# The scan pass of a vision state-space block: softplus in pairs, u*D as a matmul, a new order of work, and a part of x_proj moved into the pass

## The chip, the cores and the metric

The kernel runs on one core of one Trainium2 chip. The time is that of one execution on the device, in microseconds (us). The kernel before takes 10042.06 us, the median of three runs (10038.65 to 10054.98). A core has five engines that work side by side, each through its own queue of instructions in order: TensorE (PE in the profile; PEld is its weight load), VectorE (DVE), ScalarE (ACT), GpSimd (POOL), and SyncE (SP), which here only issues DMAs.

## What is computed

The reference is a selective state-space block with four scan directions on a batch of 8 images of 64 x 64 pixels, followed by a small attention and a feed-forward layer. Only the scan and what feeds it matter here. `B` is 8, `L` is 4096 pixels, `D_INNER` is 192 channels, `D_STATE` (n) is 16, `DT_RANK` is 6, `K` is 4 directions:

```python
x_dbl = jnp.einsum('bkdl,kcd->bkcl', xs, x_proj_weight)         # "x_proj": 6 + 16 + 16 rows
dts, Bs, Cs = x_dbl[:, :, :6], x_dbl[:, :, 6:22], x_dbl[:, :, 22:]
delta = jax.nn.softplus(dt_projs_weight @ dts + bias)            # [b, k, d, l]
h = h * jnp.exp(d_t[..., None] * A) + (d_t * u_t)[..., None] * b_t[:, :, None, :]
y = jnp.einsum('bkdn,bkn->bkd', h, c_t)                          # at each step of l
y = y + D[None, :, :, None] * u
```

The first three lines are abridged; the last three are the recurrence for one step, its output, and the term u*D, which is added once per direction.

## The kernel before

`vss_attn_ffn_kernel` calls three passes. `pass1` (line 266) norms the input, projects it, convolves it on VectorE and stores the result `u` to HBM (`u_d`); then `x_projection` (line 490) computes x_proj with TensorE, copies it out of PSUM and stores it to `xd_d`, and `split` (line 236) splits B and dt into three bf16 parts (`b_d`, `dt_d`). `pass3` does the norm, gate, output projection, attention and feed-forward.

`pass2` (line 542) is the scan. It works through 192 **pieces**: 4 pairs of images, in each pair 3 channel groups `c` (c = 0 and 1 are 128 channels of one image; c = 2 holds the last 64 channels of both), 4 directions `k`, and 4 chunks of T = 1024 pixels. A piece has 16 states n. For each n:

- `decay` (line 655): ACT makes `da` = exp(delta * A_n), 128x1024;
- `products` (line 694): the term delta*u*B_n is made in a PSUM tile `wide` in one of three ways, set by `WAYS` (line 55). Either PE spreads B_n over the partitions and DVE multiplies by `du`; or ACT (`scaled`, line 665) or POOL (`scaled_by_pool`) multiplies the transposed `duT` by B_n, which gives `x` or `xg`, and PE transposes that into `wide`;
- `scan` (line 718): one DVE instruction runs the recurrence along the 1024 pixels and writes `h`;
- for every two n: `times_c` (line 757), where POOL multiplies `h` by a loaded, broadcast tile `c`, and `sum_over_n` (line 771), where PE adds the result into the PSUM tile `acc`.

`prepare` (line 573) readies a piece: loads of `xdt`, `xb` and `u`, the B transposes, `delta` by a softplus on ACT, `du` on POOL, `duT`. Softplus and the exponential lie in different activation tables, so ACT loads a table before a softplus and another after it. For direction 0, `sum_over_n` starts `acc` with u*D: ACT multiplies (`ud`), PE transposes.

The order on each engine is fixed when the kernel is built. `weave` (line 142) takes generators that yield (engine, cost, delay, slots), keeps a clock per engine, and always emits the step that can begin first by those written costs; ties go to the lower rank (`lead` in the list of units). `room` (line 550) is the number of buffers of each kind: 3 `da`, 3 `h`, 3 `x`, 3 `wide`, 6 `c`.

The batches from `LATE` = 5 on are split during pass 2, in between (`late_split`). All of x_proj lies in pass 1; its last batch has half of its PSUM copies on DVE.

Of the kernel before, what the change touches and what calls it, by code (L numbers as in the profile page):

```python
# [33 lines left out]
F32 = mybir.dt.float32  # L34
# [20 lines left out]
WAYS = [([2, 5, 6, 8, 11, 12, 14, 15], [3, 7]), ([2, 3, 7, 9, 14], [0, 5, 12])]  # L55
NS = 3

LATE = 5
GRP = 512
# [40 lines left out]
@with_exitstack  # L100
def vss_attn_ffn_kernel(ctx: ExitStack, tc: tile.TileContext, g: dict, out: bass.AP):
    nc = tc.nc
    consts = ctx.enter_context(tc.tile_pool(name="consts", bufs=1))
    dram = ctx.enter_context(tc.tile_pool(name="scratch", bufs=1, space=DRAM))

    ident = consts.tile([P, P], F32, name="ident")
    make_identity(nc, ident)
    mhalf = consts.tile([P, NBLK], F32, name="mhalf")
    nc.vector.memset(mhalf, -0.5)


    u_d = [[dram.tile([DI, L], F32, name=f"u_d{b}_{o}") for o in range(2)] for b in range(NB)]

    y_d = [[dram.tile([L, DI], F32, name=f"y_d{b}_{o}") for o in range(2)] for b in range(NB)]
    z_d = [dram.tile([DI, L], F32, name=f"z_d{b}") for b in range(NB)]
    xd_d = [[dram.tile([2 * NXD, L], F32, name=f"xd_d{b}_{o}") for o in range(2)] for b in range(NB)]

    b_d = [[dram.tile([2, NS, N, L], BF16, name=f"b_d{b}_{o}") for o in range(2)] for b in range(NB)]
    dt_d = [[dram.tile([2, NS, R, L], BF16, name=f"dt_d{b}_{o}") for o in range(2)] for b in range(NB)]

    engines = [InOrder(tc, e) for e in (nc.tensor, nc.vector, nc.scalar, nc.gpsimd)]
    fixed, load_dt_w = scan_constants(tc, g, consts, dram, ident)
    pass1(tc, g, load_dt_w, ident, mhalf, engines, u_d, z_d, xd_d, b_d, dt_d)
    pass2(tc, g, ident, engines, fixed, u_d, xd_d, b_d, dt_d, y_d)
    pass3(tc, g, ident, mhalf, engines, y_d, z_d, out)


class Slots:


    def __init__(self, count):
        self.count, self.taken, self.ends = count, 0, {}

    def when(self):

        return 0.0 if self.taken < self.count else self.ends.get(self.taken + 1 - self.count)
# [99 lines left out]
def split(engines, pool_of, cost, src, row, rows, pieces, at, dst):  # L236

    act, pool, sp = engines
    wide, used = GRP, rows * pieces
    yield "sp", 0.7, 4.0  # L240
    bq = pool_of.tile([P, wide], F32, name="bq")
    src = src[row : row + rows].rearrange("r (s t) -> (r s) t", s=pieces)
    sp.dma_start(bq[0:used], src[:, at : at + wide])
    yield "act", 0.6
    bs = pool_of.tile([P, NS, wide], BF16, name="bs")
    act.copy(bs[0:used, 0, :], bq[0:used])
    yield "pool", cost
    pool.tensor_sub(bq[0:used], bq[0:used], bs[0:used, 0, :])
    yield "act", 0.6
    act.copy(bs[0:used, 1, :], bq[0:used])  # L250
    yield "pool", cost
    pool.tensor_sub(bs[0:used, 2, :], bq[0:used], bs[0:used, 1, :])
    yield "sp", 0.9
    half = used // 2
    for k2 in range(2):
        to = dst[k2].rearrange("e n (s t) -> (n s) e t", s=pieces)[:, :, at : at + wide]
        sp.dma_start(to, bs[half * k2 : half * (k2 + 1)])
# [8 lines left out]
def pass1(ctx, tc, g, load_dt_w, ident, mhalf, engines, u_d, z_d, xd_d, b_d, dt_d):  # L266
# [28 lines left out]
    w_xp = wp.tile([P, 3, 2, P], F32, name="w_xp")  # L295
# [194 lines left out]
    def x_projection(b, o, q):  # L490
# [15 lines left out]
        by_dve = b == NB - 1 and q % 2 == 1  # L506
        end = yield ("dve" if by_dve else "act"), 0.6 if o == 0 else 0.8
# [4 lines left out]
        (dve.tensor_copy if by_dve else act.copy)(dst, src)  # L512
# [10 lines left out]
    for pair in range(NB // 2):  # L523
        batches = (2 * pair, 2 * pair + 1)
        for b in batches:
            units += [("stats", statistics(b, q)) for q in range(NG)]
            units.append(("norm", group_norm(b)))
            units += [("proj", projection(b, q)) for q in range(NG)]
        for c in ORDER:
            units.append(("conv", convolution(pair, c)))  # L530
        for b in batches:
            for o in range(2):
                units += [("xproj", x_projection(b, o, q)) for q in range(NG)]
                if b < LATE:
                    units += [("split", after(("xd", b, o), split((act, pool, sp), two, 4.4, xd_d[b][o], *w))) for w in splits(b, o, b_d, dt_d)]
# [6 lines left out]
def pass2(ctx, tc, g, ident, engines, fixed, u_d, xd_d, b_d, dt_d, y_d):  # L542
# [5 lines left out]
    one = ctx.enter_context(tc.tile_pool(name="p2one", bufs=1))  # L548
    two = ctx.enter_context(tc.tile_pool(name="p2two", bufs=2))
    room = {"c": 6, "da": 3, "h": 3, "x": 3, "wide": 3, "xg": 1, "ud": 1, "acc": 1}  # L550
# [8 lines left out]
    done, counts, made, ys, carry = {}, {}, {}, {}, {}  # L559
# [13 lines left out]
    def prepare(at):  # L573
# [10 lines left out]
        yield "sp", 2.5, 3.0  # L584
        xdt = one.tile([2 * NS * NS * R, T], BF16, name="xdt")
        queue = sp if at else pool
        for j in range(2):
            for m in range(NS):
                row = (j * NS + m) * NS * R
                queue.dma_start(xdt[row : row + NS * R, :], dt_d[2 * pair + j][o][k2].rearrange("s r t -> (s r) t")[:, cols])  # L590
        if at > 0:
            yield "sp", 1.5, 3.0
# [18 lines left out]
        yield "pe", 0.9, 0.2, slots["wide"]  # L611
        pd, slot = take("wide", [P, T])
        for q in range(0, T, GRP):
            pe.matmul(pd[:, q : q + GRP], dt_w[:, c, k, :], xdt[:, q : q + GRP], start=True, stop=True)

        end = yield "act", 3.6, 0.2
        delta = two.tile([P, T], F32, name="delta")
        act.activation(delta, pd, AF.Softplus, bias=dt_b[:, c // 2, k : k + 1])
        slots["wide"].release(slot, end)
        made[at] = [xb, u, delta, None, None, bT]  # L620
        done["delta", at] = end
        end = yield "pool", 2.37, 0.2
        du = two.tile([P, T], F32, name="du")
        pool.tensor_mul(du, delta, u)
        made[at][3] = du
# [6 lines left out]
        made[at][4] = two.tile([P, NT, P], F32, name="duT")  # L632
        act.copy(made[at][4], pt)
        slots["wide"].release(slot, end)
        done["duT", at] = end

    def late_split(b, o, which):

        yield "scans", 0
        yield from split((act, pool, sp), one, 1.25, xd_d[b][o], *which)  # L640
        one_more(("split", b), 6, 0.0)

    def load_c(at, m):
        pair, c, k, pc = pieces[at]
        parts = chunk_rows(pair, c)
        end = yield "sp", 0.5 * len(parts), 6.0, slots["c"]
# [8 lines left out]
    def decay(at, n):  # L655
# [3 lines left out]
        end = yield "act", 1.06, 0.2, slots["da"]  # L659
        da, slot = take("da", [P, T])  # L660
        act.activation(da, made[at][2], AF.Exp, scale=a_neg[:, c // 2, k, n : n + 1])
# [3 lines left out]
    def scaled(at, n):  # L665
# [3 lines left out]
        x, (_, _, _, _, duT, bT) = None, made[at]  # L669
        for i in range(0, NT, 2):  # L670
            cost = 0.6 if c < 2 else 1.0
# [9 lines left out]
    def scaled_by_pool(at, n):  # L681
        pair, c, _, _ = pieces[at]
        yield "duT", at
        end = yield "pool", 2.0 if c < 2 else 2.2, 0.2, slots["xg"]
        x, slot = take("xg", [P, NT, P])
        _, _, _, _, duT, bT = made[at]
# [7 lines left out]
    def products(at, n):  # L694
# [3 lines left out]
        if n in by_act or n in by_pool:  # L698
            yield "x", at, n
            end = yield "pe", 1.3, 0.2, slots["wide"]  # L700
# [5 lines left out]
        else:  # L706
            yield "du", at
            end = yield "pe", 0.7, 0.2, slots["wide"]
# [4 lines left out]
            end = yield "dve", 1.22, 0.0  # L713
            dve.tensor_mul(dbu, made[at][3], dbu)
# [3 lines left out]
    def scan(at, n):  # L718
# [6 lines left out]
        if n % 2 == 0:  # L725
            end = yield "dve", 2.26, 0.2, slots["h"]
            made["h", at, n // 2] = take("h", [P, 2, T])
            done["begun", at, n // 2] = 0.0
        else:
            yield "begun", at, n // 2  # L730
            end = yield "dve", 2.26, 0.2
# [39 lines left out]
    def sum_over_n(at, m):  # L771
# [10 lines left out]
        if m == 0 and k == 0:  # L782
            yield "delta", at
            yield "act", 1.05, 0.2, slots["ud"]
            ud, slot = take("ud", [P, T])
            act.mul(ud, made[at][1], dsum[:, c // 2 : c // 2 + 1])
            end = yield "pe", 1.2, 0.0, slots["acc"]
            made["acc"] = take("acc", [P, NT, P])
            add(ud, True, False)
            slots["ud"].release(slot, end)  # L790
# [10 lines left out]
        for i in range(2):  # L801
# [3 lines left out]
            else:  # L805
                end = yield "pe", 1.2, 0.0
# [5 lines left out]
    def take_acc(at):  # L812
# [11 lines left out]
        if k >= 2 and at % NPC == NPC - 1:  # L824
            yield "sp", 2.0, 6.0
# [13 lines left out]
    for at, (pair, c, k, pc) in enumerate(pieces):  # L839
# [5 lines left out]
        add("prep", 8, prepare(at))  # L845
        for n in range(N):
            if n % 2 == 0:
                add("c", 12, load_c(at, n // 2), n)
            add("da", 2, decay(at, n), n)
            if n in by_act:  # L850
                add("x", 5, scaled(at, n), n)
            elif n in by_pool:
                add("xg", 4, scaled_by_pool(at, n), n)
            add("dbu", 1, products(at, n), n)
            add("scan", 0, scan(at, n), n)
            if n % 2 == 1:
                if at % NPC < NPC - 1:
                    add("carry", -2, carries(at, n // 2), n)
                add("term", 0, times_c(at, n // 2), n)
                add("sum", -4, sum_over_n(at, n // 2), n)  # L860
        add("acc", 0, take_acc(at), N)
    last = [(b, o, w) for b in range(LATE, NB) for o in range(2) for w in splits(b, o, b_d, dt_d)]
    units += [("split", 5 * N * (i + 1), late_split(*which)) for i, which in enumerate(last)]
    weave(units, {"prep": 1, "c": 1, "da": 2, "x": 1, "xg": 1, "dbu": 2, "scan": 2, "carry": 1, "term": 1, "sum": 1, "acc": 1, "split": 1}, done)
# [301 lines left out]
```

## Time and profile before

| what | value |
|---|---|
| median of three runs | 10042.06 us |
| the profiled execution | 10032.78 us, span 10031.0 us |
| first scan starts (pass 1 until here) | 713.87 us |
| the last scan ends, pass 3 follows | 9313.4 us |
| DVE / ACT / POOL / PE busy, whole span | 95 / 92 / 90 / 74% |
| one piece, c = 0 or 1 (pair 1, c = 1: 703.4 us for 16) | 43.96 us |
| one piece, c = 2 (pair 1: 741.6 us for 16) | 46.35 us |

A stage of 16 pieces (one pair and one c) is cut at the end of the 16th scan of its last piece. In the page's list of groups, "busy" is the time in which at least one instruction of the group runs, and "mean" the time of one from start to end; where an engine starts an instruction before the last one has quite ended, the first is less than count times mean. "Idle" is the time just before the group's instructions in which the engine did nothing, with what ended it.

### The profile page before, as it was taken

To read this page: it belongs to the slowest core of one execution; us is meant where nothing else is said; L and a number is where in the kernel's file an instruction comes from. 1 tells how busy PE (TensorE), PEld (TensorE's weight loads), DVE (VectorE), ACT (ScalarE), POOL (GpSimd) and SP (SyncE) were. 2 spreads that over 40 slices of the span, in tenths; PEclk is the share of its full clock that TensorE was granted. 3 is DMA by queue.
4 is the path that set the end of the run, shared out by engine and by line. 5 is a ranking of instruction groups with operands and counts; after the bars stand their busy time and mean duration, and the time that the engine had idled before them with its cause. 6 is when DMAs were issued, how large, how long until landed. Compare 5 with 4: busy or idle time off the path is not lost.

```text
span 10031.0 us, 152994 instructions
## 1 busy us (share of the span) xinstructions
PE 7446.5 (74%) x52384; PEld 6168.3 (61%) x52384; DVE 9534.5 (95%) x7601; ACT 9182.1 (92%) x20692; POOL 9000.1 (90%) x2911
## 2 busy tenths in 40 slices
PE   7767777777777777777777777777777777777677
PEld 3336666666656666666666666666666666665566
DVE  7879999999999999999999999999999999999798
ACT  5669999999999999999999999999999999999687
POOL 1539999999999999999999999999999999999676
PEclk8889999998998999989999989999989999989898
DMA  5766676689986666799966766899866666999653
GB/s 166 234 212 216 223 237 222 227 212 205 209 223 213 224 221 213 223 209 204 212 215 216 232 209 221 220 203 204 223 209 226 216 215 223 211 204 209 186 171 104
DMA packets 932233, 2111.70 MB, mean 211 GB/s; under 512 B 274603, under 2 KB 422860, under 8 KB 929922
## 3 DMA queue, kind: packets, MB, share of 16 engines
q1 hardware_dynamic: 928650, 2100.57, 74.0%
q8 instruction: 419, 6.86, 0.3%
q14 instruction: 356, 2.92, 0.1%
q0 software_dynamic: 432, 0.94, 0.0%
q10 hardware_dynamic: 2376, 0.40, 0.0%
HBM read 1925.98 MB, written 175.66 MB: 210 GB/s over the span
## 4 chain that ended last, share of the span: by engine, by line
DVE 31%; ACT 29%; issue 15%; PE 13%; POOL 8%; DMA 3%; SPq 1%; DVEq 0%; ACTq 0%; POOLq 0%
DVE h L91 21%; ACT x L91 11%; ACT da L91 11%; POOL c L91 6%; PE acc L91 6%; DVE wide L91 5%; PE wide L91 3%; ACT L91 2%; ACT y L91 1%; DVE u L91 1%; PE pa L91 1%; ACT delta L91 1%; PE px L91 1%; DMA xd_d<-xd 1%; POOL xg L91 1%
## 5 line engine op out<-in xcount | busy, mean ns | idle before, releaser
L91 POOL TENSOR_TENSOR c<-c,h 128x2048 f32<-128x2048 f32 x1536 | 6960.6, 4558 | 293.2 <-issue 134.2
L91 DVE TENSOR_TENSOR_SCAN h<-da,carry,wide 128x1024 f32<-128x1024 f32 x2304 | 5267.9, 2332 | 135.1 <-PE wide L91 35.7
L91 ACT ACTIVATE x<-duT,bT 128x128 f32<-128x128 f32 (+1 forms) x13312 | 3969.8, 368 | 2.0
L91 PE MATMUL acc<-ident,c 128*128 128x128 f32 x24576 | 3419.1, 297 | 594.4 <-POOL c L91 587.9
L91 ACT ACTIVATE da<-delta,a_neg 128x1024 f32<-128x1024 f32 x3072 | 3512.7, 1144 | 318.0 <-DVE h L91 305.8
L91 PEld LDWEIGHTS acc<-ident,c 128*128 128x128 f32 x24576 | 3102.5, 154 | 1031.9 <-POOL c L91 921.7
L91 PE MATMUL wide<-ident,x 128*128 128x128 f32 x10752 | 1553.0, 290 | 650.4 <-DVE h L91 604.8
L91 PEld LDWEIGHTS wide<-ident,x 128*128 128x128 f32 x10752 | 1301.4, 149 | 845.0 <-ACT x L91 393.0
L91 DVE TENSOR_TENSOR_SCAN h<-da,wide 128x1024 f32<-128x1024 f32 x768 | 1713.1, 2271 | 41.5 <-PE wide L91 9.8
L91 DVE TENSOR_TENSOR wide<-du,wide 128x1024 f32<-128x1024 f32 x1280 | 1543.9, 1207 | 39.7 <-PE wide L91 39.2
L91 PE MATMUL wide<-xb,sel 96*128 96x512 bf16 x2560 | 820.2, 404 | 685.6 <-DVE h L91 671.0
L91 POOL TENSOR_TENSOR xg<-duT,bT 128x512 f32<-128x512 f32 (+1 forms) x640 | 895.2, 1414 | 26.5 <-PE wide L91 13.3
L91 PEld LDWEIGHTS <-sel 96*128 96x128 bf16 x2560 | 232.2, 102 | 867.0 <-DVE h L91 614.8
L91 PE MATMUL wide<-ident,xg 128*128 128x128 f32 x3584 | 482.3, 279 | 118.5 <-DVE h L91 116.7
L91 ACT ACT_TABLE_LOAD x386 | 495.2, 1283 | 25.9 <-DMA w_kv<-in_bqkv 19.2
L91 PEld LDWEIGHTS wide<-ident,xg 128*128 128x128 f32 x3584 | 411.4, 144 | 148.4 <-issue 108.4
L91 POOL TENSOR_TENSOR du<-delta,u 128x1024 f32<-128x1024 f32 x192 | 457.8, 2384 | 7.7 <-DMA u<-u_d 7.7
L91 DVE SCALAR_TENSOR_TENSOR u<-xpad,conv_w,u 128x4096 f32<-128x4096 f32 x96 | 454.5, 4734 | 1.9
L91 PE MATMUL px<-u,w_xp 128*128 128x512 f32 x512 | 253.4, 635 | 57.5 <-ACT u L91 42.2
L91 POOL TENSOR_TENSOR bq<-bq,bs 128x512 f32<-128x512 f32 (+1 forms) x48 | 125.7, 2623 | 162.7 <-ACT bs L91 123.7
L91 ACT COPY y<-acc 128x1024 f32<-128x1024 f32 x192 | 192.4, 1002 | 77.8 <-PE acc L91 77.6
L91 PE MATMUL wide<-ident,du 128*128 128x128 f32 x1536 | 206.5, 278 | 69.3 <-DVE h L91 34.9
(142 smaller groups left out, 5835.6 us busy)
## 6 DMA issues: line engine op xcount, KB each, us to landing
c<-xd_d SPq DMA_DIRECT2D x1024, 1024.0 KB
c<-xd_d SPq DMA_DIRECT2D x1024, 512.0 KB
u<-u_d SPq DMA_DIRECT2D x127, 512.0 KB
xdt<-dt_d SPq DMA_DIRECT2D x1146, 36.0 KB
xb<-b_d SPq DMA_DIRECT2D x382, 96.0 KB
u<-u_d SPq DMA_DIRECT2D x128, 256.0 KB
zs<-z_d SPq DMA_DIRECT2D x128, 256.0 KB
y_d<-y SPq DMA_DIRECT2D x24, 1024.0 KB
```

Of the source, the lines that this page charges most:

```text
L91: ins = getattr(self.engine, op)(*args, **kwargs).ins
```

## The change

1. `deltas_of` takes softplus out of `prepare` and makes it for two pieces together (`SOFT` = 2), so that a pair of table loads serves two pieces; the first piece is alone. While the pair is open, no `da` is started (`held`). `delta` gets 3 buffers, `xdt` 2.
2. u*D: instead of ACT's multiply and a transpose, PE multiplies `u` by a diagonal matrix `d_diag`, which DVE makes once.
3. `WAYS`: for c = 0 and 1 other n, with the same counts (8 by ACT, 2 by POOL, 6 by DVE). For c = 2, ACT takes 6 instead of 5, POOL 3, DVE 7 instead of 8.
4. Costs, delays and leads given to `weave` change; `products` gets lead 2 instead of 1 and, with `scan`'s lead unchanged, may be placed before an earlier scan. A load of `c` now counts 3.9 on SP, a store of `y` 7.5. Buffers: `da` 4, `x` 4, no `ud`.
5. x_proj of batch 7 (`LATE_X`) moves from pass 1 into pass 2 (`late_x_projection`): 16 units, each with three loads of `ux`, two matmuls in a `wide` tile, one ACT copy and a store. No PSUM copy of x_proj is left on DVE.
6. Memory: the scan's constants and `w_xp` move to a pool that ends before pass 3; pass 2's pools are opened in another order, with the `y` tiles last.

```diff
-WAYS = [([2, 5, 6, 8, 11, 12, 14, 15], [3, 7]), ([2, 3, 7, 9, 14], [0, 5, 12])]
+WAYS = [([4, 6, 7, 9, 10, 12, 14, 15], [2, 11]), ([3, 8, 9, 12, 14, 15], [2, 6, 13])]
+SOFT = 2
+LATE_X = 7
...
-    room = {"c": 6, "da": 3, "h": 3, "x": 3, "wide": 3, "xg": 1, "ud": 1, "acc": 1}
+    three = ctx.enter_context(tc.tile_pool(name="p2three", bufs=SOFT + 1))
+    room = {"da": 4, "h": 3, "x": 4, "xg": 1, "c": 6, "wide": 3, "acc": 1}
...
+    one = ctx.enter_context(tc.tile_pool(name="p2one", bufs=1))
+    d_diag = one.tile([P, 2, P], F32, name="d_diag")
+    for ty in range(2):
+        dve.tensor_scalar(d_diag[:, ty, :], ident, dsum[:, ty : ty + 1], None, ALU.mult)
...
+    def deltas_of(first):
+        group = range(first, min(first + SOFT, len(pieces))) if first else range(1)
+        if first > 1:
+            yield "scans", first - 2
...
+        for i, at in enumerate(group):
+            pair, c, k, pc = pieces[at]
+            yield "pe", 0.9, 0.2, slots["wide"]
+            pd, slot = take("wide", [P, T])
+            for q in range(0, T, GRP):
+                pe.matmul(pd[:, q : q + GRP], dt_w[:, c, k, :], pds[i][:, q : q + GRP], start=True, stop=True)
+            end = yield "act", 2.3, 0.2
+            slots["da"].held = i < len(group) - 1
+            deltas[at] = three.tile([P, T], F32, name="delta")
+            act.activation(deltas[at], pd, AF.Softplus, bias=dt_b[:, c // 2, k : k + 1])
+            slots["wide"].release(slot, end)
+            done["delta", at] = end
+    def late_x_projection(b, o, q):
+        yield "scans", 0
...
+        yield "pe", 1.5, 0.2, slots["wide"]
+        px, slot = take("wide", [P, T])
+        for i, ty in enumerate((0, 1 + j)):
+            pe.matmul(px[:, 0:GRP], w_xp[:, ty, o, :], ux[:, i, :], start=i == 0, stop=i == 1)
+        end = yield "act", 0.58, 0.2
...
-            end = yield "dve", 1.22, 0.0
-            dve.tensor_mul(dbu, made[at][3], dbu)
+            end = yield "dve", 1.22, 0.1
+            dve.tensor_mul(dbu, made[at][2], dbu)
...
-            act.mul(ud, made[at][1], dsum[:, c // 2 : c // 2 + 1])
-            end = yield "pe", 1.2, 0.0, slots["acc"]
-            add(ud, True, False)
+            yield "pe", 1.9, 0.0, slots["acc"]
+            for i in range(NT):
+                pe.matmul(
+                    made["acc"][0][:, i, :], made[at][1][:, i * P : (i + 1) * P], d_diag[:, c // 2, :],
...
-        add("prep", 8, prepare(at))
+        if at == 0 or at % SOFT == 1:
+            add("soft", 14, deltas_of(at))
+        add("prep", 12, prepare(at))
...
-            add("da", 2, decay(at, n), n)
+            add("da", 1, decay(at, n), n)
-            add("dbu", 1, products(at, n), n)
+            add("dbu", 2, products(at, n), n)
-                add("term", 0, times_c(at, n // 2), n)
-                add("sum", -4, sum_over_n(at, n // 2), n)
+                add("term", -2, times_c(at, n // 2), n)
+                add("sum", -6, sum_over_n(at, n // 2), n)
```

## The prediction, made before the changed kernel was run

> **What bounds the kernel now.** I read the page's busy shares first (DVE 95%, ACT 92%, POOL 90% of the span). These are averages, so the next view was the busy time by stage, cut at the ends of the 16-piece stages; columns are the window, its length, then PE, PEld, DVE, ACT and POOL busy, the granted clock, the DMA share and GB/s.
>
> ```profile
> 3569.40:4272.80 703.40, 539.51 (x3970) 461.80 (x3969) 685.57 (x353) 677.81 (x1480) 676.21 (x178) 0.92 0.69 219
> 4272.80:5014.40 741.60, 537.75 (x3785) 453.91 (x3786) 726.50 (x387) 694.76 (x1740) 713.08 (x239) 0.90 0.93 209
> ```
>
> Divided by 16, a piece of c = 0 or 1 takes 43.96 us, of which DVE is busy 42.85, ACT 42.36, POOL 42.26. A piece of c = 2 takes 46.35: DVE 45.41, ACT 43.42, POOL 44.57. DVE is the bound in both, but two others stand within 4% of it, so what DVE gains can be taken only as far as the next engine lets it.
>
> What DVE loses is told by its own timeline and its waits (us in total, times, longest), the latter over 900 to 9250 us:
>
> ```profile
> 3659.26 1.21 DVE L91 TENSOR_TENSOR wide<-du,wide 128x1024 f32<-128x1024 f32 x1
> 3660.57 4.58 DVE L91 TENSOR_TENSOR_SCAN h<-da,carry,wide 128x1024 f32<-128x1024 f32 x2
> 3665.07 1.21 DVE L91 TENSOR_TENSOR wide<-du,wide 128x1024 f32<-128x1024 f32 x1
> 3666.19 13.53 DVE L91 TENSOR_TENSOR_SCAN h<-da,carry,wide 128x1024 f32<-128x1024 f32 x6
> 3679.63 1.21 DVE L91 TENSOR_TENSOR wide<-du,wide 128x1024 f32<-128x1024 f32 x1
> 3680.94 2.35 DVE L91 TENSOR_TENSOR_SCAN h<-da,carry,wide 128x1024 f32<-128x1024 f32 x1
> ```
> ```profile
> DVE h L91 <- PE wide L91: 43.3, 44, 2.7
> DVE wide L91 <- PE wide L91: 26.2, 26, 1.1
> ```
>
> The product at 3659.26 is followed by the scan that reads it 1.31 us later, the one at 3679.63 also 1.31; the product at 3665.07 is followed after 1.12 us by a scan that reads another tile. A product right before its own scan thus costs 0.19 us more. Real waits, for PE above all, sum to 81 us in all rows of that view, 0.43 us a piece.
>
> The transition from pass 1, again DVE's timeline:
>
> ```profile
> 629.55 15.07 DVE L91 SCALAR_TENSOR_TENSOR u<-xpad,conv_w,u 128x4096 f32<-128x4096 f32 x3
> 655.87 0.69 DVE L91 COPY xd<-px 76x512 f32<-76x512 f32 x1 [11.24 <-PE px L91]
> ...
> 700.01 0.69 DVE L91 COPY xd<-px 76x512 f32<-76x512 f32 x1 [3.36 <-DMA xd_d<-xd]
> 711.60 2.36 DVE L91 TENSOR_TENSOR wide<-du,wide 128x1024 f32<-128x1024 f32 x2 [10.90 <-PE wide L91]
> 713.87 8.81 DVE L91 TENSOR_TENSOR_SCAN h<-da,wide 128x1024 f32<-128x1024 f32 x4
> ```
>
> The convolution ends at 644.6 and the first scan starts at 713.9: 69 us with 5.5 us of copies in them, while x_proj of batch 7 runs out through PE, PSUM copies and stores.
>
> **What the Trainium skill says.** ScalarE: Activation LUTs, What ACT_TABLE_LOAD costs: a load takes about 1283 ns and a drain of some 1380 ns more. The trace agrees on the first (1283 ns mean) and not on the second: the load at 3595.76 of 1.28 us is followed by a softplus at 3597.05. I use 1.28 us. VectorE: DVE Perf Modes, The DRAIN you can't avoid: a semaphore between chained operations "costs nothing extra". The trace shows otherwise for a scan behind its own product, the 0.19 us above, and the measurement decides. Perfetto Trace Analysis, Optimizing Scalar/DVE Operations: where DVE is saturated, offloading to Scalar may help. For c = 2 the change does this, with ACT at 93.7% of the stage, so the trace says how little room there is.
>
> **The products' order (edit 4).** In the built programs, of 1280 products before, 1047 stand right before their own scan; after, 213 of 1216. For c = 0 and 1 alone it is 610 before and 152 after, of 768 each. 458 x 0.19 = 87 us over 128 pieces, 0.68 a piece. Against it: a product placed ahead needs its `wide` tile filled by PE one scan (2.24 us start to start) earlier, and `wide` still has 3 buffers. The refill takes 0.6 to 1.0 us after a scan frees the tile, but 16 acc transposes of 1.9 us can stand before it. So some of the gain may return as waits for PE; the bounds are 0 and 0.68 + 0.43 (all waits gone too). POOL stands at 42.26 in pair 1 and at 694.37/16 = 43.40 and 690.15/16 = 43.13 in pair 0 (the late splits), so pair 0 gets less. I take 0.65 for 96 pieces (62) and 0.25 for the 32 of pair 0 (8): **-70 us**, from -20 to -100.
>
> **Softplus by pairs, u*D on PE, for c = 0 and 1 (edits 1, 2).** ACT loses half of its table loads (32 in a stage of 16 pieces: 16 x 1.28 / 16 = 1.28 a piece) and `ud` (4.6/16 = 0.28). It goes from 42.36 to 40.8 while DVE needs some 43.2: nothing directly, since ACT isn't the bound; the cover is that DVE is later anyway. PE's 8 matmuls with `d_diag` replace 8 transposes of the same shape (0.28 us for such `acc<-y,ident` matmuls against 0.35), 48 times: nothing. `d_diag` itself is two short DVE instructions in the idle 644.6 to 713.9.
>
> **c = 2 (edits 1 to 3).** DVE: one product fewer (start to start 1.12 to 1.31) and 376 of 437 close pairs gone (376 x 0.19 / 64 = 1.1 a piece): need about 44.0. POOL: unchanged, 44.57. ACT: before 43.42; a further n is 16 multiplies of 128x64, of which eight in a row take 1.91 us (2501.13 to 3.04), so +3.82; table loads -1.28; `ud` 4.5/16 = -0.28. Sum **45.68**: ACT becomes the bound, 0.67 below today's 46.35. What idle time ACT will have no trace shows. The bounding engine today has 0.94 (46.35 - 45.41), half of it the close pairs that ACT doesn't have; ACT is tied to DVE through 4 `da` and to PE through 4 `x`. From 0.2 to 1.2; I take 0.6, giving 46.3: 64 x -0.05 = **-3 us**, from -29 to +35.
>
> **The transition (edits 5, 6).** Gone from it are 32 matmuls, 16 copies and 16 stores of x_proj. What is late next: ACT's silu of the last convolution (647.7 to 651.6) and four copies `ut`, 1.96 us each, of which the third still waits for the store of the first (it began at 663.9); the fourth ends about 668. Then SP issues the last 2 MB store of `u`, at about 671. In the built program the first `h` tile lies on that `u` tile, so the first scan waits for the landing, and so do the first loads of `c`. Before, the store was issued at 677.78, and the load of `c` that waits for it went out at 693.19: 15.4 us. So the first scan comes at about 687 instead of 713.9. First softplus and `du` (POOL queues their DMAs behind the last split at 655.2) are ready at some 673 and don't decide. `c` lands a few us later; three `h` tiles let DVE run six scans, some 17 us, without it. **-27 us**, from -15 to -35.
>
> **Moved into the pass.** 16 times: three loads and a store on SP's queue (before, SP mostly waits for free `c` tiles: 5988 us of its waits end with PE acc), two PE matmuls (0.63 us each), an ACT copy of 0.58 us, a `wide` tile for some 2 us. 16 x 0.58 = 9 us of ACT in pair 0, which has 1.3 us a piece free and gains 1.6. Nothing while ACT has room; without it, 9 us; PE and `wide` may cost DVE a few tenths each, in pair 0's reduced gain.
>
> **The end.** Pass 3's first memsets waited 23.3 us for the last store of `y` (to 9336.7); with `y` at the end of memory they wait for scans. But the first load of pass 3's `yo` still stands on SP's queue behind the four stores (9322.55 to 9332.45). Only constants and the table load come sooner: **-3 us**, 0 to -5. SP's loads of `c` and `xdt` in their new order: nothing; the six `c` tiles hold 33 us of work, and DMA is at 0.93 for c = 2, whose bytes don't change.
>
> **Sum.** -70 - 3 - 27 - 3 = -103 us against the profiled execution: 10032.78 becomes 9930. The median of the runs shown is 9 us above that execution, so I forecast 10042 - 103 = 9939, rounded to **9940 us**. About 0.2% (20 us) is what a measurement of this kernel can tell from no change.
>
> **Rivals.**
> 1. *Thin gain.* The waits for `wide` take back the products' gain, or ACT idles 1.2 us for c = 2. For it: `wide` has no more buffers, and PE waits for it (DVE h) 1479 us in all. Against: those are PE's waits, DVE's own are 81. Products at -20 and c = 2 at +20 give 10042 - 20 + 20 - 30 = 10012.
> 2. *Slower: a drought of exponentials.* Between the last `da` and the first `da` around a pair of softpluses ACT's new order holds, by the durations here, a median of 7.7 us of other work (two loads, two softpluses, 6 to 12 multiplies, carries); around a single softplus it was 5.6 us (3595.05 to 3600.65). DVE lives off the ready `da`: four last 4 x 2.24 us plus products, 10.7 us. If ACT enters with two or three ready, as it may for c = 2 where it is the bound, or if the second softplus waits for its `wide` tile with `da` barred, DVE stalls. There are 96 pairs: at 103/96 = 1.07 us a pair the gain is gone, and from 1.28 us it is slower by more than can be doubted. At 1.6 us: 10042 - 103 + 154 = 10093. Against it: for c = 0 and 1 ACT has over 2 us a piece free and should enter with four.
> 3. *More.* Most of DVE's waits go too (0.3 x 128 = 38), and ACT idles only 0.2 for c = 2 (26): 9940 - 64 = 9876.
>
> **How the numbers follow.** Forecast 0.58 (9895 to 9985), more 0.12, thin gain 0.17, slower 0.13. The thin case reaches from -0.5% to no change: 0.10 of it faster, 0.07 within 0.2%. So faster 0.80, same 0.07, slower 0.13. The range reaches up through the thin gain and down to the "more" case: 9875 to 10030.
>
> **What would show it.** By stage: 16 pieces of pair 1 to 3, c = 0 or 1, in about 693 us, with DVE's idle time down from 1.1 to some 0.5 a piece and its waits for PE not above 100 us; c = 2 in about 741 us with ACT busy 731, DVE below 710; first scan near 687, behind the store of `u`; about 195 table loads in place of 386. It is wrong if the waits `DVE h <- ACT da` grow from 2 us to over 60 (rival 2), if `DVE <- PE wide` doubles (rival 1), or if the c = 2 stage exceeds 755 us.

## The result and the profile after

The changed kernel takes 10027.43 us, the median of 15 runs (10014.30 to 10046.44), beside 10040.26 us for the kernel before on the same chip (15 runs). The ratio is 0.9988, with a 95% interval from 0.9980 to 0.9995: about 13 us faster, where 103 were forecast. The profiled execution took 10019.36 us. In this section times are those of the two profiled executions, one of each kernel. Differences between runs further below are differences of ratios times 10038 us; such a difference is uncertain by some 15 us, because the interval of a ratio reaches 7 to 16 us to either side.

The busy time by stage, of the kernel after, for the two stages shown of before (columns: window, its length, then PE, PEld, DVE, ACT and POOL busy, clock, DMA share, GB/s):

```profile
3584.10:4287.20 703.10, 532.80 (x4000) 457.75 (x4000) 681.95 (x354) 660.19 (x1470) 684.18 (x185) 0.94 0.70 222
4287.20:5019.70 732.50, 545.83 (x3904) 466.40 (x3904) 700.14 (x370) 717.39 (x1959) 712.17 (x240) 0.91 0.94 211
```

DVE is busy 42.6 us a piece for c = 1 (42.85 before) and 43.8 for c = 2 (45.4 before), ACT 41.3 and 44.8. DVE did get less to do in both; for c = 2 that work went to ACT. The same view over the whole scan, from the first scan to the last, first of before, then of after:

```profile
713.90:9313.40 8599.50, 6387.45 (x46793) 5458.04 (x46794) 8394.10 (x4351) 8193.36 (x18759) 8284.19 (x2402) 0.92 0.77 216
```
```profile
687.40:9299.40 8612.00, 6428.14 (x47610) 5536.46 (x47609) 8259.17 (x4287) 8143.56 (x19565) 8281.33 (x2401) 0.93 0.78 217
```

This pair holds the case: DVE's busy time falls by 134.9 us, and its idle time rises from 205.4 to 352.8, by 147.4. The scan is 12.5 us longer than before, and only the transition in front of it is a gain.

The idle time is of two kinds. Counted over DVE's instructions in the two traces, 120.2 of the 205.4 us before lie in 1066 gaps of at most 0.15 us, 1041 of them right behind a product; after, such gaps are 231 with 25.4 us. So DVE saved 134.9 us of work and 94.8 us of gaps, 229.7 in all, and its longer waits rose by 242.2 us, from 85.2 to 327.4. The saving is what the forecast's prices give: 834 close pairs fewer at 0.19 us and 64 products fewer at 1.12 us are 230 us. The waits took all of it.

By kinds of stage (16 pieces each, cut at the ends of the 16th scans):

| stages | before | after | difference |
|---|---|---|---|
| until the first scan | 713.9 | 687.4 | -26.4 |
| c = 0 and 1 with late work (pair 0, and pair 1 c = 0) | 2112.9 | 2145.2 | +32.3 |
| the other five of c = 0 and 1 | 3519.5 | 3509.5 | -10.0 |
| the four of c = 2 | 2967.1 | 2957.3 | -9.8 |
| pass 3 | 717.6 | 718.2 | +0.6 |

After the change the late work lasts until 4052 us: four of its 18 splits fall into the first of the "other five", and the c = 2 stage of pair 0 has late work too. That stage is 8.8 us longer than before; the other three of c = 2 are 18.6 us shorter together.

What DVE waits for after the change (us in total, times, longest), over 900 to 9250 us, the window of the lines shown of before:

```profile
DVE h L93 <- PE wide L93: 176.1, 132, 9.1
DVE wide L93 <- PE wide L93: 94.3, 105, 3.5
DVE h L93 <- ACT da L93: 24.2, 26, 3.6
```

The waits for a filled `wide` tile went from 69.5 to 270.4 us (the expectations below count from 720 us and say 278). Exponentials are not scarce. One such wait, in DVE's timeline of the kernel after (start, length, engine, instruction, and in brackets the idle time before and what ended it):

```profile
5129.81 9.04 DVE L93 TENSOR_TENSOR_SCAN h<-da,carry,wide 128x1024 f32<-128x1024 f32 x4
5140.12 2.35 DVE L93 TENSOR_TENSOR_SCAN h<-da,carry,wide 128x1024 f32<-128x1024 f32 x1 [1.28 <-PE wide L93]
5142.39 1.21 DVE L93 TENSOR_TENSOR wide<-du,wide 128x1024 f32<-128x1024 f32 x1
```

and PE's in the same stretch:

```profile
5134.42 1.09 PE L93 MATMUL wide<-ident,xg 128*128 128x128 f32 x8 [1.14 <-DVE h L93]
5137.10 0.60 PE L93 MATMUL wide<-xdt,dt_w 108*128 108x512 bf16 x2
5138.90 1.09 PE L93 MATMUL wide<-ident,x 128*128 128x128 f32 x8 [1.20 <-DVE h L93]
5139.82 0.60 PE L93 MATMUL wide<-xb,sel 96*128 96x512 bf16 x2
```

The scan that ends at 5138.85 frees the tile; PE fills it from 5138.90 on; the next scan is the one that needs it, and starts at 5140.12. The fill before it on PE (5137.10) had gone to a softplus.

### The profile page after: what moved, and what is told of

Same layout as the page of the kernel before. It is cut to its first block, busy times and chain, and to the rows that moved or that the text cites. A ratio compares the mean times of both kernels' runs of the same rounds, so it can differ in the third digit from the quotient of the medians.

```text
span 10017.6 us, 155167 instructions
## 1 busy us (share of the span) xinstructions
PE 7462.9 (74%) x53152; PEld 6241.3 (62%) x53152; DVE 9397.2 (94%) x7531; ACT 9126.6 (91%) x21486; POOL 9005.3 (90%) x2911
## 4 chain that ended last, share of the span: by engine, by line
DVE 28%; ACT 19%; issue 19%; PE 16%; POOL 10%; DMA 7%; SPq 1%; DVEq 0%; POOLq 0%; ACTq 0%
DVE h L93 19%; POOL c L93 8%; ACT x L93 8%; ACT da L93 7%; PE wide L93 7%; PE acc L93 6%; DVE wide L93 4%; DMA c<-xd_d 3%; DVE u L93 1%; PE px L93 1%; PE pa L93 1%; POOL xg L93 1%; ACT y L93 1%; ACT L93 1%; DMA xd_d<-xd 1%
## 5 line engine op out<-in xcount | busy, mean ns | idle before, releaser
L93 ACT ACTIVATE x<-duT,bT 128x128 f32<-128x128 f32 (+1 forms) x14336 | 4197.4, 367 | 13.1 <-PE wide L93 11.7
L93 PEld LDWEIGHTS acc<-ident,c 128*128 128x128 f32 x24576 | 3050.0, 152 | 797.9 <-POOL c L93 663.4
L93 PE MATMUL wide<-ident,x 128*128 128x128 f32 x11264 | 1602.8, 289 | 704.8 <-DVE h L93 668.4
L93 PEld LDWEIGHTS wide<-ident,x 128*128 128x128 f32 x11264 | 1335.2, 148 | 952.5 <-issue 393.4
L93 DVE TENSOR_TENSOR wide<-du,wide 128x1024 f32<-128x1024 f32 x1216 | 1462.8, 1209 | 125.5 <-PE wide L93 97.0
L93 PE MATMUL wide<-xb,sel 96*128 96x512 bf16 x2432 | 762.6, 399 | 353.6 <-DVE h L93 331.8
L93 PE MATMUL wide<-ident,xg 128*128 128x128 f32 x3584 | 549.9, 304 | 301.5 <-DVE h L93 276.0
L93 PEld LDWEIGHTS wide<-ident,xg 128*128 128x128 f32 x3584 | 463.9, 158 | 373.1 <-issue 214.1
L93 POOL TENSOR_TENSOR du<-delta,u 128x1024 f32<-128x1024 f32 x192 | 456.8, 2379 | 41.3 <-DMA u<-u_d 23.4
L93 ACT COPY carry<-h 128x2 f32<-128x2 f32 x1152 | 213.9, 186 | 150.1 <-DVE h L93 145.1
```

The costliest lines, as they stand in the source:

```text
L93: ins = getattr(self.engine, op)(*args, **kwargs).ins
```

## The experiments

Each run was timed in rounds against the kernel before.

**Products at their own scans, all else in place.** The order of every other engine is kept; the product is only held back on DVE.

```diff
-            dve.tensor_mul(dbu, made[at][2], dbu)
+            late_mul[at, n] = partial(dve.tensor_mul, dbu, made[at][2], dbu)
...
+        if (at, n) in late_mul:
+            late_mul[at, n]()
         dve.tensor_tensor_scan(h[:, way], da[:, way], dbu[:, way], init, ALU.mult, ALU.add)
```

> The changed kernel with only this different: each of DVE's 1216 products is issued right before the scan that reads it; the order of everything else, on every engine, stays. Close pairs rise from 213 to 1216. Theory of the forecast (the 0.19 us of a close pair is lost time on a DVE that bounds the stage): 1003 x 0.19 = +190 us, or, counting only that the waits which grew stay as they are, at least +130. Rival (the gain was handed back as waits for the PSUM tiles `wide`, because a product ahead of its time asks for its tile one scan sooner): the waits of DVE for PE fall from 278 to under 150 us and the time changes by -20 to +60 us.

Measured 1.0153 (1.0139 to 1.0167): 166 us slower than the changed kernel, 0.165 us for each of the 1003 products put back, with the change in waits included. In the traces work and gaps alone grow by 203 us, 0.20 us a product. The waits of this run:

```profile
DVE h L93 <- PE wide L93: 177.2, 130, 5.3
DVE h L93 <- ACT da L93: 45.2, 37, 4.6
DVE wide L93 <- PE wide L93: 34.8, 40, 2.5
```

The scans' waits for PE stayed; only those of the products fell (from 94.3), and the waits for `da` rose by 21 us. The price of a close pair in the forecast was right, in this order of the other engines. So the rival of this run fell: the products placed ahead do pay 166 us, but with them put back the changed kernel is 153 us slower than the kernel before.

**The lead alone, on the kernel before**, and the lead undone on the kernel after. With the lead goes the delay written for a product (0.1 in the change, 0.0 before), and the list then plans the whole order anew:

```diff
-            end = yield "dve", 1.22, 0.0
+            end = yield "dve", 1.22, 0.1
...
-            add("dbu", 1, products(at, n), n)
+            add("dbu", 2, products(at, n), n)
```

> The kernel before with only the products' lead 2 and their delay 0.1, the order planned anew: 387 close pairs instead of 1047. Theory of the forecast (0.16 us a close pair, nothing against it): -106 us, waits for PE up to 120. New theory (placing products ahead brings the waits for the refill by itself): DVE's waits for PE rise from 70 to over 200 us, and the time is between -40 and +100 us.

Measured 1.0095 (1.0079 to 1.0110): 95 us slower than before. DVE's waits in that run:

```profile
DVE wide L91 <- PE wide L91: 164.7, 210, 2.4
DVE h L91 <- PE wide L91: 55.5, 63, 6.9
DVE wide L91 <- ACT x L91: 21.7, 22, 2.2
```

660 close pairs went, worth 109 us at 0.165; the waits for PE rose from 69.5 to 220.2 and those for `x` from 1.5 to 37.8, and the kernel lost. This is the part done alone: planning products ahead brings the waits with it.

> The changed kernel with the list's lead of the products back at 1 and their delay at 0, so that the whole order is planned anew around it: 624 close pairs instead of 213. Theory A (a close pair costs 0.16 us, as the run with every product at its own scan showed, and the rest of the order stays as good or bad): 411 x 0.16 = +66 us, waits of DVE for PE as before the undoing, about 280. Theory B (with three `wide` tiles a product ahead makes DVE wait out PE's refill, so an order that isn't ahead is worth as much): waits of DVE for PE fall below 200 and the time is within 20 us of the changed kernel.

Measured 1.0033 (1.0023 to 1.0044), 45 us slower than the changed kernel, waits for PE 240.3. That is between the two theories: the lead gains in the changed kernel, less than its close pairs are worth, and undoing it doesn't bring the waits back to 70. Other edits of the order hold them up too.

**The late work.** All of x_proj back in pass 1:

```diff
-LATE_X = 7
+LATE_X = NB
```

> The changed kernel with the x_proj of batch 7 back in pass 1, all its PSUM copies on ACT; pass 2 keeps only the 18 splits as late work. Theory of the forecast (the moved work costs nothing in pass 2, the transition gains 27): the first scan goes back to 708 to 720 us and the whole gets 20 to 30 us slower. Rival (each unit is 4 matmuls of 0.59 us, not 2, on a PE that DVE waits for, and it spreads the splits over 73 pieces; stages with late work are 0.8 to 1.0 us a piece slower than stages without): the stages 1 to 5 get 25 to 50 us shorter, which gives back the transition's gain: -20 to +10 us in all.

Measured 0.9991 (0.9985 to 0.9998), 3 us from the changed kernel, with the first scan at 712.9 instead of 687.4 and the scan itself 8594.4 us long instead of 8612.0. The total fits the rival: what the transition gains is lost again later. The splits stay spread out here too: the last ends at 3634 us, after 1873 us in the kernel before and 4052 us in the changed one.

**The loads of xb.** A third buffer, filled one piece sooner:

```diff
+        for nxt in (0, 1) if at == 0 else (at + 1,):
...
+                ahead[nxt] = three.tile([KB, T], BF16, name="xb")
...
+        xb = ahead[at]
...
-        xb = two.tile([KB, T], BF16, name="xb")
```

In the changed kernel, PE's waits have this line, which before had no counterpart in the scan:

```profile
PE wide L93 <- DMA xb<-b_d: 43.1, 15, 8.1
```

The worst case, in the timelines of SP, PE and DVE of the changed kernel:

```profile
9141.30 18.29 SPq L93 DMA_DIRECT2D c<-xd_d  x14
9161.36 3.71 SPq L93 DMA_DIRECT2D xb<-b_d  x2
9167.06 2.77 SPq L93 DMA_DIRECT2D u<-u_d  x2
```
```profile
9169.71 1.91 PE L93 MATMUL acc<-ident,c 128*128 128x128 f32 x16
9179.74 0.38 PE L93 MATMUL wide<-sel,xb 96*128 96x32 bf16 x8 [8.12 <-DMA xb<-b_d]
9179.95 1.95 PE L93 MATMUL wide<-ident,xg 128*128 128x128 f32 x8
```
```profile
9168.33 4.57 DVE L93 TENSOR_TENSOR_SCAN h<-da,carry,wide 128x1024 f32<-128x1024 f32 x2
9182.04 2.35 DVE L93 TENSOR_TENSOR_SCAN h<-da,carry,wide 128x1024 f32<-128x1024 f32 x1 [9.13 <-PE wide L93]
```

PE reaches the transposes of B for the next piece before their operand has landed, 18 us after its issue; 14 loads of `c` had gone out just ahead of it. The `xg` transposes that DVE needs come next on PE and start only at 9179.95, and DVE idles 9.13 us.

> The changed kernel with a third buffer for `xb`, whose load is issued one piece sooner on SP; u and everything else in its place. The trace shows PE standing 43 us, 15 times and up to 8.1 us, for this load, mostly for c = 2, with DVE starved just after (9.1 us at 9182). Theory (these waits end up on DVE): PE's waits for `xb` go to under 5 us and the time falls by 20 to 45 us, nearly all of it for c = 2. Rival (the transposes of B aren't what DVE waits for, or `u`, which is still late, takes their place): less than 10 us either way.

Measured 0.9966 (0.9954 to 0.9979), 22 us faster than the changed kernel, a little more than the uncertainty; PE's waits for `xb` are 1.6 us. The theory put nearly all of it into c = 2; in the profiled executions, which differ by 6 us only, the c = 2 stages are 8.5 us shorter, so where the rest lies isn't shown.

**Softplus one at a time**, for the second rival of the forecast:

```diff
-SOFT = 2
+SOFT = 1
```

> The changed kernel with one softplus at a time (SOFT = 1): 386 table loads instead of 196 (+1.28 us of ACT a piece), no drought of exponentials around a pair. Theory of the forecast (ACT doesn't bound c = 0 and 1, and bounds c = 2): nothing for c = 0 and 1, and up to +1.28 x 64 = 82 us for c = 2, so 0 to +82 in all. Rival (the pair's drought of 7.7 us stalls DVE): faster by 10 to 60 us, with fewer waits of DVE for ACT da. New reading (DVE waits for `wide`, and ACT's x arrives a little later): c = 2 slower by 10 to 40 us, the rest within 10.

Measured 1.0051 (1.0039 to 1.0064), 63 us slower. DVE's waits for `da` fall from 24.2 to 14.7 us, those for PE rise to 336.5. There is no drought worth the name; the pairs pay. By stages, in the profiled executions, 43 us are lost in c = 2 and 33 in c = 0 and 1, where both the forecast and the new reading expected almost nothing. The changed kernel has 196 table loads; the kernel before and this run have 386.

**PE's prices in the list** as before:

```diff
-            end = yield "pe", 1.0, 0.2, slots["wide"]
+            end = yield "pe", 1.3, 0.2, slots["wide"]
...
-            end = yield "pe", 0.5, 0.2, slots["wide"]
+            end = yield "pe", 0.7, 0.2, slots["wide"]
```

> The changed kernel with PE's prices for a filled `wide` tile as before (1.3 for transposes instead of 1.0, 0.7 instead of 0.5), products still at lead 2: 245 close pairs. In the trace a refill runs 1.28 us from the end of a scan to the start of the next one for transposes and 0.7 to 1.1 for the spread of B, so the new prices are too low and the list places DVE's work where `wide` isn't full yet. Theory C (the low prices make the waits): DVE's waits for PE fall from 278 to under 180 us, and the time falls by 40 to 100 us. Rival (the refill has to be waited for in any order with three tiles and two products ahead): waits within 40 us of 278, time within 30 us of the changed kernel or, as the list's own clock has it, slower by up to 130.

Measured 1.0040 (1.0028 to 1.0053), 52 us slower, waits for PE 271.9, as the rival has it. The prices don't make the waits.

**Which engine binds.** Work taken off one engine, with every order kept:

```diff
+            w = T // 2 if n == 1 else T
-            dve.tensor_mul(dbu, made[at][2], dbu)
+            dve.tensor_mul(dbu[:, 0:w], made[at][2][:, 0:w], dbu[:, 0:w])
```

> The kernel before with the product of n = 1 made on half its columns (the other half of B isn't multiplied by delta*u): about 0.58 us a piece less for DVE, 192 x 0.58 = 111 us, every order as it was. Theory (before, DVE bounds every stage): faster by 80 to 115 us. Rival (another engine or the refills of `wide` already bound it): less than 50.

> The changed kernel with the product of n = 1 made on half its columns (the other half of B isn't multiplied by delta*u): about 0.58 us a piece less for DVE, 111 us in all, every order as it was. Theory of the forecast (DVE still bounds c = 0 and 1, ACT bounds c = 2): faster by 60 to 75, all of it for c = 0 and 1. New theory (after the change DVE has to wait for the refill of `wide`, and time taken off DVE only lengthens the wait): faster by less than 50 us against the changed kernel.

A half product takes 678 ns instead of 1212, so 0.53 x 192 = 102 us were taken away. Before: 0.9935 (0.9922 to 0.9947), 65 us faster, 0.64 of it. After: 0.9949 (0.9936 to 0.9961), 39 us faster than the changed kernel, 0.38 of it. The first lies between its two theories: even there DVE's longer waits grew, from 85 to 117 us in the trace. The second fits the new theory. Less of DVE's work turns into time than before.

The same for POOL (in `times_c`) and for ACT (in `scaled`):

```diff
-        pool.tensor_mul(c2, c2, h2)
+        w = T // 2 if m == 3 else T
+        pool.tensor_mul(c2[:, :, 0:w], c2[:, :, 0:w], h2[:, :, 0:w])
```
```diff
-                for j, (part, _, _) in enumerate(chunk_rows(pair, c)):
+                for j, (part, _, _) in enumerate([(slice(0, P), 0, 0)] if n == 9 else chunk_rows(pair, c)):
```

> The changed kernel with one of eight products of h and C in a piece made on half its columns, so POOL has 2.3 us a piece less to do (the other half of that term is left as loaded); every order stays. Theory E (POOL, busy 42.2 of 43.8, is a bound beside DVE: h tiles come free late): 0.5 us a piece or more, so -100 us or more. Rival (POOL waits for DVE, not the other way): within 20 us of the changed kernel.

> The changed kernel, in which ACT for c = 2 and n = 9 makes 8 multiplies of 128x128 with the B of the first image instead of 16 of 128x64 with each image's own (so that one term is wrong for the second image): 1.9 us a piece less for ACT, 64 x 1.9 = 122 us, c = 0 and 1 and every order as they were. Theory of the forecast (ACT bounds c = 2 after the change, DVE needs 44.0): c = 2 falls from 46.2 to about 44.8 a piece, 60 to 110 us in all. Rival (the refills of `wide` and late loads bound c = 2): less than 40 us.

POOL, whose busy time fell by 408 us: 0.9986 (0.9979 to 0.9992), 2 us faster. ACT, whose busy time for c = 2 fell by 1.3 us a piece (81 us): 0.9982 (0.9976 to 0.9989), 6 us. Neither can be told from nothing; both rivals were right, and neither engine is the bound.

And c = 2 shared out as before:

```diff
-([3, 8, 9, 12, 14, 15], [2, 6, 13])]
+([2, 3, 7, 9, 14], [0, 5, 12])]
```

> The changed kernel with c = 2 shared out as before: ACT 5, POOL 3, DVE 8 of 16 n, the order planned anew. Theory of the forecast (this part is worth next to nothing: ACT at 45.7 in place of DVE at 45.4 as the bound): within 25 us of the changed kernel, with ACT busy about 41.0 and DVE about 45.0 of a c = 2 piece. Rival (moving that n to ACT is the change's gain for c = 2): slower by 40 to 80 us.

Measured 1.0060 (1.0047 to 1.0072), 72 us slower, all in the c = 2 stages (47.2 instead of 46.0 us a piece in pairs 1 to 3), where DVE is busy 45.0. There, too, the rival was right.

**The refill itself.** First a kernel that makes only one of eight transposes into `acc` (in `sum_over_n`) and so leaves out most of the sum; then, in both kernels, the refill issued twice, of either kind:

```diff
-            for i in range(NT):
+            for i in range(NT if first else 1):
                 pe.matmul(
                     made["acc"][0][:, i, :], term[:, i * P : (i + 1) * P], ident, is_transpose=True,
```
```diff
-            for q in range(0, T, GRP):
+            for q in (0, 0, GRP, GRP):
                 pe.matmul(dbu[:, q : q + GRP], spread(n, c), xb[:, q : q + GRP], start=True, stop=True)
```
```diff
-            for i in range(NT):
+            for i in (*range(NT // 2), *range(NT)):
                 pe.transpose(dbu[:, i * P : (i + 1) * P], x[:, i, :], ident)
```

> The changed kernel with one of eight transposes that add a term into `acc` (the first term of direction 1 whole): 7/8 of the sum over n is left out of seven blocks in eight, everything else and every order stays. It takes most of the work that stands ahead of the refills of `wide` on PE's queue. Theory D (PE's queue is congested, and refills come late behind `acc`): DVE's waits for PE fall to under 120 us and the time by 100 us or more. Rival (the refill itself, which starts only when a scan frees the tile, is what DVE waits for): waits stay above 180, and the time falls by less than 60.

> The kernel before with each spread of B into `wide` issued twice (4 matmuls of 128x512 instead of 2, the same values written again), every order as it was: 1280 refills longer by about 0.43 us at full clock, 550 us if all of it lay on DVE's path. Theory (before, a tile is refilled well ahead of its product and the refill has slack): slower by less than 150 us, under 0.12 us for each refill. Rival (no slack in either order): 300 us or more.

> The changed kernel with each spread of B into `wide` issued twice, every order as it was: 1216 refills longer by about 0.43 us at full clock, 520 us if all of it lay on DVE's path. Theory (with products ahead two of three tiles hold finished products, and DVE waits out the refill of the third): slower by 250 us or more, at least twice what the kernel before loses by the same edit. Rival (the refills have as much slack as before, and DVE's waits come from elsewhere): within 60 us of what the kernel before loses.

> The kernel before with four of the eight transposes of x or xg into a `wide` tile issued twice (same values written again), every order as it was: 10 refills a piece (8 for c = 2), 1792 in all, longer by 0.44 us at full clock, 790 us if all of it lay on DVE's path. Theory (before, these refills have slack, their waits are 43 us): slower by less than 150 us. Rival (none): 300 us or more.

> The changed kernel with four of the eight transposes of x or xg into a `wide` tile issued twice, every order as it was: 10 refills a piece (9 for c = 2), 1856 in all, longer by 0.44 us at full clock, 817 us if all of it lay on DVE's path. Theory (the slack of these refills is what the new order spent: 181 of DVE's 278 us of waits stand there): slower by 200 us or more, and by at least twice what the kernel before loses. Rival (they have as much slack as before): within 60 us of what the kernel before loses.

| run | ratio (95%) | against its own base | mean clock |
|---|---|---|---|
| acc_thin | 1.0039 (1.0026 to 1.0052) | +51 us | 0.713 |
| refill_twice_before | 1.0054 (1.0042 to 1.0067) | +54 us | 0.931 |
| refill_twice | 1.0026 (1.0014 to 1.0037) | +38 us | 0.940 |
| transposes_before | 1.0039 (1.0026 to 1.0051) | +39 us | 0.938 |
| transposes_twice | 0.9969 (0.9959 to 0.9980) | -19 us | 0.946 |

The clock of the first two kernels is 0.914 (before) and 0.918 (after). Taking work from PE made the kernel slower. Adding work to the changed one cost 38 us for the spread of B, and for the transposes (PE is busy 6921 us of the scan instead of 6428) it was faster by 19 us, hardly more than the uncertainty. The theory that the new order had spent the slack of its refills fell: longer refills cost the changed kernel no more than the kernel before, as the rivals of its two runs said. Nor does the first run test congestion, because the clock went with the work. The group of the `x` transposes in acc_thin, and the same in the changed kernel (count, busy us, mean ns, idle before):

```profile
L93 PE MATMUL wide<-ident,x 128*128 128x128 f32 x11131 | 2101.0, 352 | 1047.1 <-DVE h L93 984.6 <-ACT x L93 48.8 <-ACT da L93 5.6
```
```profile
L93 PE MATMUL wide<-ident,x 128*128 128x128 f32 x11208 | 1594.5, 289 | 701.0 <-DVE h L93 664.7 <-ACT x L93 26.1 <-ACT da L93 6.7
```

**A version that beats both.** `xb` and `u` both one piece ahead in three buffers; x_proj of batch 7 and its weights back in pass 1, which frees the room. In `prepare`:

```diff
+        for nxt in (0, 1) if at == 0 else (at + 1,):
...
+                xb = three.tile([KB, T], BF16, name="xb")
...
+                u = three.tile([P, T], F32, name="u")
...
+                ahead[nxt] = xb, u
+        xb, u = ahead[at]
```

> The changed kernel with the x_proj of batch 7 back in pass 1 (and the weights `w_xp` in pass 1's pool, which frees the room), and with third buffers for `xb` and `u`, both loaded one piece sooner. Theory (late loads cost some 17 us by `xb` and POOL's 23 us of waits for u a few more; x_proj is neutral): 20 to 45 us faster than the changed kernel, so 0.9945 to 0.997 of the kernel before. Rival (u and x_proj add nothing, or the loads ahead come in the way of those of c): no better than 0.997.

Measured 0.9958 (0.9945 to 0.9970): 42 us faster than before, 30 faster than the changed kernel. The 8 us beyond `xb` alone can't be told from nothing. Its scan, in the profiled execution, which at 9979.97 us is 17 us below the median of this run:

```profile
713.80:9264.60 8550.80, 6364.38 (x47546) 5490.10 (x47546) 8255.84 (x4287) 8131.34 (x19543) 8285.10 (x2402) 0.93 0.77 217
```

DVE has the work of the changed kernel and 295.0 us of idle time instead of 352.8. POOL's 23.4 us of waits for `u`, over 900 to 9250 us, are gone.

## Why the prediction was wrong

The measured time lies just below the upper end of the stated range, which had been drawn that far for the first rival; of the 103 us of the sum, 90 are missing.

- **The products' order, -70: this step failed, in what it set against the gain.** Unit price and count held: the whole saving of 230 us is in the trace. The text saw that a product ahead needs its tile one scan sooner with three tiles, then took 0.03 us a piece of loss for it in 96 pieces. In its place, DVE's waits for `wide` rose from 69.5 to 270.4 us. That is more than the doubling that the forecast had named as the sign of its first rival, which was given 0.17. In the other five stages of c = 0 and 1, where 0.65 a piece or 52 us were forecast, the gain is 10.0 us, 0.12 a piece. In the three with late work, where 18 us were forecast, 32.3 us are lost. The lead alone, on the kernel before, brings 151 us of such waits and costs 95 us net. That three tiles are too few for this order is the likely reason, but no run shows it.
- **Moved x_proj, "nothing": failed.** Each unit is four matmul instructions of 593 ns, not two. Put back, the scan is 17.6 us shorter, in one execution each; the changed kernel's own 15 runs reach from 10014 to 10046 us. The splits, which before ended by piece 26, last until piece 74; with x_proj put back they still last until 3634 us, so most of that spread comes from other edits of the order. What the units and what the spread cost isn't shown apart.
- **SP's new order, "nothing": failed by 22 us**, the late `xb`; together with `u` and x_proj, 30. Which of the edits on SP made `xb` late was not tried.
- **u*D on PE, "nothing": its count was off.** The trace has 768 matmul instructions `acc<-d_diag,u` of 273 to 552 ns, 16 for each of 48 pieces and not 8, where the kernel before had 384 transposes of `ud`. What that costs was not tried.
- **c = 2, -3: the sum came near (-9.8) by luck, and its reason was wrong.** It adds 18.6 us of gain in pairs 1 to 3 and 8.8 us of loss in pair 0. ACT at 44.8 of 45.8 us doesn't bind: 81 us less work gave 6. Most of DVE's relief of 1.65 us a piece went into its waits: its idle time there is 2.0 to 2.3 in pairs 1 to 3, 0.9 before. Nor were close pairs half of that 0.9, as the forecast took it: the small gaps made up 0.79 us of it. The new share of c = 2 is worth 72 us within this order.
- **The transition, -27: the number was right (-26.4) by luck, the path was another.** SP's last store of `u` went out at 679.1, not 671, and the loads of `c` that wait behind it at 687.0, 7.9 us later and not 15.4. The first scan starts 2.27 us after the first of two products, as it did before, so it waited for the products. They came through the chain that the forecast had ruled out: the fourth `ut` copy stood in front of the first softplus on ACT, and `du` and the products follow it.

```profile
674.20 1.93 ACT L93 COPY ut<-u 128x1024 f32<-128x1024 f32 x1 [8.78 <-DMA u_d<-ut]
676.73 1.91 ACT L93 COPY ut<-u 128x1024 f32<-128x1024 f32 x1 [0.61 <-DMA u_d<-ut]
678.65 1.28 ACT L93 ACT_TABLE_LOAD   x1
679.95 1.11 ACT L93 ACTIVATE delta<-wide,dt_b 128x1024 f32<-128x1024 f32 x1
681.15 2.35 POOL L93 TENSOR_TENSOR du<-delta,u 128x1024 f32<-128x1024 f32 x1 [7.38 <-DMA u_d<-ut]
685.17 2.36 DVE L93 TENSOR_TENSOR wide<-du,wide 128x1024 f32<-128x1024 f32 x2 [22.99 <-issue]
687.44 4.46 DVE L93 TENSOR_TENSOR_SCAN h<-da,wide 128x1024 f32<-128x1024 f32 x2
```

- **Pairs of softplus: right that they cost nothing** (the second rival, with 24.2 us of waits for `da` where over 60 would have shown it), though undoing them costs 63, so within this order they were worth more than the 0 put down.
- **The end, -3:** pass 3 is 0.6 us longer.

What stays open: which of the other edits of the order (the leads of `da`, `xg`, `c` and the sums, the n of `WAYS`) keep the waits at 240 us when the lead of the products is undone. They weren't tried one by one. Why doubled transposes do no harm to the changed kernel is open too. The higher clock (0.946) may be the reason, but doubled spreads of B, at 0.940, cost 38 us.

## What to carry to other kernels

Where engines pass a few tiles around in a fixed order, a saving on the busiest engine counts only as far as its waits don't grow: add busy and idle time over the same stretch before and after, and split the idle time into small gaps and waits. Here the saving was 230 us, as priced, and the added waits were 242. A part of a jointly planned order that is undone alone tells little of its net worth: five of the six parts undone here cost 45 to 166 us each, in a change that gains 13 in all. It takes the part done alone on the kernel before. And an early place in an in-order queue for something whose load is late stalls all that stands behind it, as the transposes of B did with the refills of `wide`.

## What the runs showed of the hardware

The granted TensorE clock goes with the work on PE. The Trainium skill says so (TensorE: Matmul & The Clock Gate, Part 1: The HAM clock gate: "the default state is throttled, and activity releases the throttle"), and the runs agree: 0.713 with most of the transposes into `acc` gone, 0.918 in the changed kernel, 0.940 and 0.946 with more work. Work taken from PE changed the length of its other instructions as well: the mean of an `x` transpose went from 289 to 352 ns when most of those into `acc` were gone. So that run didn't test PE's queue alone. In one kernel, eight transposes into a tile last 1.09 us at 5138.90, where the granted clock is 1.00, and 1.95 us at 9179.95, where it is 0.50, after PE had stood 8.12 us.
